# Keys of a cross-attention block: the order of the sums that end the keys' stage, and the power in two parts

## The chip, the cores and the metric

The kernel runs on one core of one Trainium2 chip. The metric is the time of the whole kernel on the device, in microseconds (us): the median over several runs. [...] Engines wait for each other by semaphores.

## What is computed

One block of a perceiver-like network on 128 rows `x` and 12544 context rows of width 512. Most of the time goes to the cross-attention to the context, of which this is the core:

```python
kvx = einsum('bsi,oi->bso', cond, w_kv_x)        # cond: the context, 12544 x 512
kx, vx = split(kvx, 2, axis=-1)                  # keys, values: 8 groups of 128 each
kx = ln(kx.reshape(b, sc, g, d), kxln_w, kxln_b) # a norm over the 128 of each key
xout = gqa(qx, kx, vx)                           # 16 query heads, 2 per group, softmax over the context
```

Around it stand a second attention of x to itself (with rounding to 8 bits), a projection of both, a causal self-attention, and a mixture of 32 experts with 8 chosen per row. The change touches only the cross-attention.

## The kernel before, in words

**Chunks.** The context is worked off in 25 chunks (0 to 24) of 512 tokens; chunk 12, in the middle, has 256. For each chunk there is a keys' stage (keys of the chunk into `KT`, with the outputs of the chunk before it on PE in between) and a values' stage (values into `V`, with the scores of the chunk in between). So on PE the order is: keys of chunk c with outputs of chunk c-1, values of chunk c with scores of chunk c, and so on. "Whole" chunks, all but 0 and 12, use the routine that is changed, `chunk_of`, for both stages (`k_chunk`, `v_chunk`).

**Products.** The 2x2 block product of mixed weights and mixed tokens is formed with seven products instead of eight (numbers 0 to 6), after Winograd's variant of Strassen. The outputs of a stage come in two units u, called the first and the second half: for the keys, groups 0 to 3 and groups 4 to 7; for the values, two sets of token tiles. Each unit has four output blocks `out(u, i, j)`. Of the seven products, 1, 3, 2 and 6 are split again by the same method into "quarters" that serve both halves at once: `pair(0, ..)` and `pair(1, ..)` are two generators of five steps each, in the banks 0, 1 and 2 of PSUM. Products 0, 5 and 4 are formed whole for each half, in a bank of their own for each half (`acc[u]`), and 0, 5 and 4 accumulate there: after each of them DVE adds the bank to its output block(s) (`add`, L332). So a bank can take its next product only when DVE has read the one before. ScalarE copies some quarters out of PSUM (`kept`, L329).

**Lower sums.** `out(u, 1, 0)` gets `out(u, 1, 1)` added on POOL (L522, one instruction for each half). The sum of product 4 writes `out(u, 1, 1)` afterwards, so it waits for that lower sum.

**The keys' norm.** After the last sum of a half, `k_sums` squares it on ScalarE (L594) and reduces the squares on DVE (L598); `k_rstd` folds the sums on DVE (L611, L617, L620) and raises to the power -0.5 on POOL (L622). The result `krs` scales the scores as ScalarE takes them out of PSUM (L941), so the first scores of a chunk can leave PSUM only when the first half's power is there. The scores' PSUM pool has three buffers.

**Other work in the queues.** POOL also mixes the next chunk's tokens (`mix_tokens`, L303 to L306, four instructions of 128x512, asked for after the last lower sum that the program has listed: `tc.issue_after(lower[0] or made)`), the finer mixtures (L445 to L448), and rescales the running outputs (L1028). DVE takes maxima of the scores (L949, L966, L976), subtracts them (L1013) and adds outputs (L1046). SP reloads the finer weights (`reload`, L432) and the context (L284).

**Order.** The program lists the stages' steps with generators: each step of `chunk_of` yields how many fills (pieces of outputs, or of scores) go after it. A build step then places the instructions on each engine; `tc.issue_after(x)` keeps what follows behind instruction x. For the keys, `keys` runs the fills and calls `k_sums` and `k_rstd`: the first half's fold is called after the first of the two closing steps, the second half's in the next stage (`after`, at g == 1).

Of the kernel before, what the change touches and what calls it, by code (L numbers as in the profile page):

```python
# [13 lines left out]
ALU = mybir.AluOpType  # L14
# [8 lines left out]
NH, G, D = 16, 8, 128  # L23
# [3 lines left out]
EPS = 1e-5  # L27
# [18 lines left out]
def block_kernel(  # L46
# [23 lines left out]
    nc = tc.nc  # L70
# [33 lines left out]
    mhalf = keep.tile([P, 16], F32, name="mhalf")  # L104
# [201 lines left out]
            lambda: eng.tensor_tensor(t4, b21, t2, ALU.subtract),  # L306
        ]

    mixed, last_mm, added, copied, lower = {}, [None], [None], [None], [None]
    aw = [[wkv[:, 0:2, o, :], wkv[:, 2:4, o, :]] for o in range(2)]  # L310
    mixed_w = (aw[0][0], aw[0][1], wsum[2], aw[1][1], wsum[0], wsum[1], aw[1][0])

# [12 lines left out]
    def bank(i):  # L325
        return (ps_kv if i < 3 else ps_kv3).tile([P, CH], F32, tag=f"kv{i}", name=f"kv{i}_ps")
# [156 lines left out]
    def chunk_of(v, c, fine, mm, view, to, pair_view, out, fills):  # L483


        def pair(p, banks):
            f = factors(c, v, p)
            return quarters(
                lambda ps, n, first: fine(f, ps, n, first), view, lambda i, j: to(p, i, j), banks
            )  # L490

        def reload(p):
            d = c if v == 0 else c + 1
            while d < NCH and not whole(d):
                d += 1
            if d < NCH and (1 - v, p) in kept_w:
                load_finer_weights(1 - v, p)

        acc = {}

        def main_part(u, i):
            if i == 0:
                acc[u] = bank((1, 3)[u])
            mm(acc[u], u, i, i == 0)
            if i == 4:
                add(out(u, 0, 1), pair_view(acc[u]))
                add(out(u, 1, 1), pair_view(acc[u]))
            else:
                add(out(u, i // 5, 0), pair_view(acc[u]))

        fills = iter(fills)
        for _ in pair(0, (1, 0, 2)):
            yield next(fills), None
        reload(0)
        extra = {1: (0, 0), 2: (1, 0), 3: (0, 5), 4: (1, 5)}
        for i, _ in enumerate(pair(1, (0, 1, 2))):
            if i in extra:
                main_part(*extra[i])
            if i == 4:
                reload(1)  # L520
                for u in range(2):
                    lower[0] = nc.gpsimd.tensor_tensor(  # L522
                        out(u, 1, 0), out(u, 1, 0), out(u, 1, 1), ALU.add
                    ).ins
            yield next(fills), None
        for u in range(2):
            main_part(u, 4)
            yield next(fills), u

    def k_chunk(c):  # L530

        h = CH // 2

        def fine(f, ps, n, first):
            for j in range(4):
                i, g = j // 2, j % 2
                nc.tensor.matmul(  # L537
                    ps[:, j * P : (j + 1) * P], lhsT=f[i][0][n][:, g * D : (g + 1) * D],
                    rhs=f[i][1][n], start=first and j == 0, stop=True, skip_group_check=True,
                )  # L540

        def mm(ps, u, i, first):
            w, x = mixed_w[i], mixed[c][i]
            for j in range(2):
                for k in range(2):
                    nc.tensor.matmul(  # L546
                        ps[:, j * h : (j + 1) * h],
                        lhsT=w[:, k, (2 * u + j) * D : (2 * u + j + 1) * D], rhs=x[:, k, :],
                        start=first and j == k == 0, stop=j == k == 1, skip_group_check=True,
                    )  # L550

        return chunk_of(
            0, c, fine, mm, lambda t: t.rearrange("p (g t) -> p g t", g=4),
            lambda p, u, v: KT[:, 4 * u : 4 * u + 4, p * h + v * P : p * h + (v + 1) * P],
            lambda t: t.rearrange("p (g t) -> p g t", g=2),
            lambda u, i, j: KT[:, 4 * u + 2 * i : 4 * u + 2 * i + 2, j * h : (j + 1) * h],
            (1, 1, 2, 1, 1, 1, 1, 1, 1, 1, 3, 2),
        )

    def v_chunk(c):  # L560

        def fine(f, ps, n, first):
            for i in range(2):
                nc.tensor.matmul(  # L564
                    ps[:, i * H // 2 : (i + 1) * H // 2], lhsT=f[i][1][n], rhs=f[i][0][n],
                    start=first and i == 0, stop=True, skip_group_check=True,
                )

        def mm(ps, v, i, first):
            w, x = mixed_w[i], mixed[c][i]  # L570
            for k in range(2):
                nc.tensor.matmul(  # L572
                    ps, lhsT=x[:, k, v * P : (v + 1) * P], rhs=w[:, k, H : 2 * H],
                    start=first and k == 0, stop=k == 1, skip_group_check=True,
                )

        return chunk_of(
            1, c, fine, mm, lambda t: t.rearrange("p (i g d) -> p i g d", i=2, d=D),
            lambda p, o, v: V[:, 2 * p + v].rearrange("p (i c g) d -> p i c g d", i=2, c=2)[
                :, :, o, :, :D  # L580
            ],
            heads, lambda v, i, j: v_out(2 * j + v, i),
            (1, 1, 2, 1, 1, 1, 1, 1, 1, 2, 2, 0),
        )

    def k_sums(c, u, pool):

        n = chunks[c][1]
        r = tmpk.tile([P, 4, CH // 32], F32, tag="sqr", name="sqr")
        for j in range(0, 4, 2):  # L590

            sq = pool.tile([P, CH // P, HS], F32, tag="s", name="sq", **({} if c else {"bufs": 1}))
            sq = sq.rearrange("p (g t) k -> p g (t k)", g=2)[:, :, :n]
            nc.scalar.activation(sq, KT[:, 4 * u + j : 4 * u + j + 2, :n], AF.Square)  # L594
            for i in range(1 if n == CH else 2):
                g = slice(j, j + 2) if n == CH else slice(j + i, j + i + 1)
                x = sq if n == CH else sq[:, i : i + 1, :]
                nc.vector.tensor_reduce(  # L598
                    r[:, g, : n // 32], x.rearrange("p g (b i) -> p g b i", i=32), AX.X, ALU.add,
                    apply_transpose=True,  # L600
                )
        return r

    def k_rstd(c, u, r):

        n, nt = chunks[c][1] // 32, chunks[c][1] // P


        w = tmpk.tile([32, 4, 4, CH // 32], F32, tag="kw", name="kw", bufs=1)
        for q in range(4):  # L610
            nc.vector.tensor_reduce(  # L611
                w[:, q, :, :n], r[32 * q : 32 * q + 32, :, :n, None], AX.X, ALU.add
            )
        ve = small.tile([P, 4, CH // P], F32, tag="kve", name="kve")
        wv = w.rearrange("p q g (t b) -> p g t b q", b=4)
        for b in range(4):
            nc.vector.tensor_reduce(  # L617
                ve[32 * b : 32 * b + 32, :, :nt], wv[:, :, :nt, b, :], AX.X, ALU.add
            )
        nc.vector.tensor_scalar(ve[:, :, :nt], ve[:, :, :nt], 1.0 / D, EPS, ALU.mult, ALU.add)  # L620
        rs = small.tile([P, 4, CH // P], F32, tag="krs", name="krs")
        nc.gpsimd.tensor_tensor(  # L622
            rs[:, :, :nt], ve[:, :, :nt],
            mhalf.rearrange("p (g t) -> p g t", g=4)[:, :, :nt], ALU.pow,
        )
        for g in range(4):
            rstds[c, 4 * u + g] = rs[:, g, :]

# [4 lines left out]
    def keys(c, fill, halves, squares):  # L633


        sums = {}
        if whole(c):
            due, given = 0, 0
            for n, unit_done in k_chunk(c):
                if unit_done is not None:  # L640
                    sums[unit_done] = k_sums(c, unit_done, squares)
                due += n
                while given < due * halves // 2:
                    next(fill)
                    given += 1
                if unit_done == 0:
                    k_rstd(c, 0, sums.pop(0))
            return sums
        for i, _ in enumerate(parts(k_unit(c, u) for u in range(2))):
            if i in (3, 7):  # L650
                sums[i // 7] = k_sums(c, i // 7, squares)
            for _ in range(halves):
                next(fill)
            if i == 6:
                k_rstd(c, 0, sums.pop(0))
        return sums
# [12 lines left out]
    with tc.tile_pool(name="pre", bufs=2) as pre, tc.tile_pool(name="pre1", bufs=1) as pre1, tc.tile_pool(  # L669
# [3 lines left out]
        for src, n in ((wqxT, 4), (wkT, 2), (wvT, 2), (wqT, 4)):  # L673
            v = src.rearrange("(k p) o -> p k o", p=P)
            stream += [v[:, :, i * H : (i + 1) * H] for i in range(n)]
        v = wprojT.rearrange("(b k p) o -> b p k o", p=P, k=NK)
# [233 lines left out]
        sums = first_sums(first_keys, sqp)  # L910
# [163 lines left out]
    for c in range(NCH):  # L1074
# [55 lines left out]
        if c + 1 < NCH:  # L1130
            fill = all_outputs()
            sums = keys(c + 1, fill, chunks[c][1] // HS, sp)
# [6 lines left out]
    with ExitStack() as rest:  # L1139
# [44 lines left out]
        c = NCH - 1  # L1184
# [329 lines left out]
```

## Time and profile before

| | us |
|---|---|
| median of 3 runs (lowest, highest) | 2200.26 (2199.98, 2200.66) |
| the profiled execution: time | 2197.91 |
| its span, first to last instruction | 2196.1 |
| PE busy | 2115.2 |
| DVE busy | 1544.2 |
| ACT busy | 936.9 |
| POOL busy | 709.5 |
| mean granted PE clock, as a share of full speed | 0.983 |

Times inside the execution are from the span's start. A line of a timeline gives start, length, engine, line, instruction, what it writes and reads, shapes, count, and in brackets the idle time before it with what ended it. A line of waits gives who waited for whom, the total, the number of times and the longest. A line of a group gives busy time and mean length in ns, and then the idle time before. A line of stretches gives from and to, then the busy time of PE, PEld, DVE, ACT and POOL, the granted clock, the share of the transfer engines, and GB/s. In the trace a whole chunk takes 76 to 78 us, and one full chunk's keys' stage runs from 850.70 to 888.28, its values' stage from there to 928.58.

### The profile page before, as it was taken

The numbers are of one execution on the slowest core, as the hardware profiler recorded it, in microseconds if no ns is written. First come the engines' busy times: TensorE is split into PE (matmuls) and PEld (weight loads), VectorE is DVE, ScalarE is ACT, GpSimd is POOL, SyncE is SP. The second block draws the span as 40 slices with busy tenths as digits, with TensorE's granted clock in tenths as the row PEclk, the third lists the DMA queues.
The fourth block names the chain that finished last, engine by engine and source line by source line (L and its number), as shares of the span: only waits on it lengthen the run. The fifth ranks groups of instructions, "written<-read, shape, count | busy, mean of one in ns | idle before, by whom it ended". The sixth has DMA issues, their size and how long they took to land.

```text
span 2196.1 us, 29775 instructions
## 1 busy us (share of the span) xinstructions
PE 2115.2 (96%) x11425; PEld 1709.5 (78%) x11425; DVE 1544.2 (70%) x2933; ACT 936.9 (43%) x1831; POOL 709.5 (32%) x888
## 2 busy tenths in 40 slices
PE   8999999999999999999999999999999999999999
PEld 4667887887887788787787887888788788776554
DVE  8787777678677767767777678777767867766311
ACT  3444454345445444444454445445434544542211
POOL 5325334324333422434334323333422433321000
PEclk9999999999999999999999999999999999999999
DMA  9311111021111111110111111111102111106693
GB/s 323 104 49 44 63 63 63 30 77 49 44 63 63 38 54 63 53 44 34 49 63 63 43 64 48 44 63 63 63 30 72 54 44 63 44 35 236 201 284 119
DMA packets 84494, 168.22 MB, mean 77 GB/s; under 512 B 4608, under 2 KB 40960, under 8 KB 84352
## 3 DMA queue, kind: packets, MB, share of 16 engines
q1 hardware_dynamic: 84064, 166.28, 22.1%
q8 instruction: 90, 1.47, 0.3%
q14 instruction: 52, 0.43, 0.1%
q10 hardware_dynamic: 288, 0.04, 0.0%
HBM read 162.90 MB, written 3.41 MB: 76 GB/s over the span
## 4 chain that ended last, share of the span: by engine, by line
PE 78%; DVE 10%; POOL 4%; ACT 4%; issue 2%; DMA 2%; SPq 0%; POOLq 0%; ACTq 0%; DVEq 0%
PE kv_ps L537 13%; PE s_ps L936 12%; PE kv_ps L564 12%; PE kv_ps L572 11%; PE o_ps L1039 10%; PE kv_ps L546 9%; PE gu_ps L1429 4%; POOL krs L622 3%; DVE sqr L598 3%; DVE KT L332 2%; PE moe_acc L1450 2%; ACT s L941 2%; PE ps_p L734 1%; PE kv_ps L366 1%; ACT sq L594 1%
## 5 line engine op out<-in xcount | busy, mean ns | idle before, releaser
L936 PE MATMUL s_ps<-qxT,KT 128*128 128x256 f32 x1568 | 391.9, 384 | 50.0 <-ACT s L941 50.0
L936 PEld LDWEIGHTS s_ps<-qxT,KT 128*128 128x128 f32 x1568 | 297.9, 192 | 152.1 <-ACT s L941 60.1
L941 ACT ACTIVATE s<-s_ps,krs 128x256 f32<-128x256 f32 x784 | 322.9, 471 | 203.6 <-PE s_ps L936 152.8
L332 DVE TENSOR_TENSOR KT<-kv_ps,KT 128x512 f32<-128x512 f32 (+1 forms) x334 | 226.6, 684 | 251.8 <-PE kv_ps L546 188.1
L1039 PE MATMUL o_ps<-V,s 128*128 128x129 f32 x3136 | 398.4, 276 | 1.3 <-ACT s L1026 0.7
L1039 PEld LDWEIGHTS o_ps<-V,s 128*128 128x128 f32 x3136 | 384.9, 192 | 9.9 <-ACT s L1026 1.4
L949 DVE TRANSPOSE_TENSOR_REDUCE mxr<-s 128x32 f32<-128x1024 f32 (+1 forms) x200 | 243.7, 1219 | 179.2 <-ACT s L941 179.2
L1026 ACT ACTIVATE s<-s 128x1024 f32<-128x1024 f32 (+1 forms) x200 | 202.4, 1038 | 121.9 <-DVE s L1013 118.5
L1028 POOL TENSOR_TENSOR ol<-ol,als 128x258 f32<-128x258 f32 x192 | 112.3, 616 | 409.5 <-ACT als L994 409.5
L1013 DVE TENSOR_TENSOR s<-s,b_ps 128x1024 f32<-128x1024 f32 (+1 forms) x200 | 232.0, 1190 | 1.7
L329 ACT COPY KT<-kv_ps 128x512 f32<-128x512 f32 (+1 forms) x196 | 112.6, 575 | 268.7 <-PE kv_ps L537 247.9
L332 DVE TENSOR_TENSOR V<-kv_ps,V 128x512 f32<-128x512 f32 x331 | 213.8, 668 | 14.4 <-PE kv_ps L564 10.9
L622 POOL TENSOR_TENSOR krs<-kve,mhalf 128x16 f32<-128x16 f32 (+1 forms) x50 | 143.0, 2860 | 246.0 <-DVE kve L620 245.9
L594 ACT ACTIVATE sq<-KT 128x1024 f32<-128x1024 f32 (+1 forms) x100 | 101.2, 1036 | 279.4 <-DVE KT L332 277.7
L522 POOL TENSOR_TENSOR KT<-KT 128x512 f32<-128x512 f32 x46 | 58.3, 1267 | 394.2 <-DVE KT L332 394.2
L546 PE MATMUL kv_ps<-mix,wsum 128*128 128x256 f32 x736 | 173.9, 379 | 0.0
L572 PE MATMUL kv_ps<-wsum,mix 128*128 128x512 f32 x368 | 172.9, 592 | 0.0
L546 PEld LDWEIGHTS kv_ps<-mix,wsum 128*128 128x128 f32 x736 | 132.9, 190 | 14.3
L329 ACT COPY V<-kv_ps 128x512 f32<-128x512 f32 x193 | 113.6, 589 | 39.7 <-PE kv_ps L564 21.6
L598 DVE TRANSPOSE_TENSOR_REDUCE sqr<-sq 128x32 f32<-128x1024 f32 (+1 forms) x104 | 117.0, 1164 | 7.9 <-ACT sq L594 7.9
L564 PE MATMUL kv_ps<-fw,fx 128*128 128x256 f32 x368 | 113.9, 464 | 1.4 <-ACT V L329 0.2
L572 PEld LDWEIGHTS kv_ps<-wsum,mix 128*128 128x128 f32 x368 | 69.9, 190 | 48.8 <-issue 44.0
(276 smaller groups left out, 3166.7 us busy)
## 6 DMA issues: line engine op xcount, KB each, us to landing
fw<-kept_w SPq DMA_DIRECT2D x88, 768.0 KB, 4.2
ctx<-in_ctxT SPq DMA_DIRECT2D x23, 1024.0 KB, 6.6
gu<-in_w SPq DMA_DIRECT2D x32, 384.0 KB, 5.1
gu<-in_v SPq DMA_DIRECT2D x32, 384.0 KB, 5.7
dn<-in_w SPq DMA_DIRECT2D x16, 768.0 KB, 5.7
w<-in_wprojT SPq DMA_DIRECT2D x8, 1024.0 KB, 5.5
w<-in_wqxT SPq DMA_DIRECT2D x4, 1024.0 KB, 11.3
w<-in_wqT SPq DMA_DIRECT2D x4, 1024.0 KB, 5.3
```

The lines of the kernel that those rows point to most:

```text
L329: copied[0] = nc.scalar.copy(dst, src).ins
L332: added[0] = nc.vector.tensor_tensor(dst, src, dst, ALU.add).ins
L537: nc.tensor.matmul(ps[:, j * P : (j + 1) * P], lhsT=f[i][0][n][:, g * D : (g + 1) * D], rhs=f[i][1][n], start=first and j == 0, stop=True, ...
L546: nc.tensor.matmul(ps[:, j * h : (j + 1) * h], lhsT=w[:, k, (2 * u + j) * D : (2 * u + j + 1) * D], rhs=x[:, k, :], start=first and j == k ...
L564: nc.tensor.matmul(ps[:, i * H // 2 : (i + 1) * H // 2], lhsT=f[i][1][n], rhs=f[i][0][n], start=first and i == 0, stop=True, skip_group_ch ...
L572: nc.tensor.matmul(ps, lhsT=x[:, k, v * P : (v + 1) * P], rhs=w[:, k, H : 2 * H], start=first and k == 0, stop=k == 1, skip_group_check=True,)
L622: nc.gpsimd.tensor_tensor(rs[:, :, :nt], ve[:, :, :nt], mhalf.rearrange("p (g t) -> p g t", g=4)[:, :, :nt], ALU.pow,)
L936: scored[0] = nc.tensor.matmul(ps[:, t - t0, :], lhsT=KT[:, g, t * P : (t + 1) * P], rhs=qxT[:, 2 * g : 2 * g + 2, :], start=True, stop=Tr ...
L941: copied[0] = nc.scalar.activation(s[:, t, :], ps[:, t - t0, :], AF.Copy, scale=rs[:, t : t + 1]).ins
L949: nc.vector.tensor_reduce(mxr[g // 4][:, g % 4, :nt, :].rearrange("p t k -> p (t k)"), s[:, :nt, :].rearrange("p t (k i) -> p (t k) i", i=32),
L1013: nc.vector.tensor_tensor(s[:, :nt, :], s[:, :nt, :], b[:, a, None, :].to_broadcast([P, nt, HS]), ALU.subtract,)
L1039: end = nc.tensor.matmul(ps[:, h, :], lhsT=s[:, t, h * S : (h + 1) * S], rhs=V[:, t, g, :], start=h == t == 0, stop=t == nt - 1, skip_grou ...
```

## The change

In `chunk_of`, for keys and values alike: the first half's product 0 is formed within the first pair of quarters (before its fourth step) and its sum after the fifth; its product 5 and the second half's product 0 are formed after the second and third step of the second pair. Then three steps close the stage: first half's product 4, second half's product 5, second half's product 4. The second half's product 5 thereby moves from before its lower sum to behind it. The banks of the two halves change places (first half bank 3, second half bank 1). In the keys the sums of the last step are placed behind the fold of the first half's squares (`folded[0]`, the last DVE instruction of `k_rstd`). `keys` calls the squares after the first and the third closing step, and the first half's fold after the second. The numbers of fills per step follow (13 steps instead of 12, the same sums: 16 and 14). In `k_rstd` the power is two instructions of two groups each instead of one of four; this holds for all chunks.

```diff
-        def main_part(u, i):
+        def product(u, i):
             if i == 0:
-                acc[u] = bank((1, 3)[u])
+                acc[u] = bank((3, 1)[u])
             mm(acc[u], u, i, i == 0)
+
+        def sums(u, i):
             if i == 4:
                 add(out(u, 0, 1), pair_view(acc[u]))
                 add(out(u, 1, 1), pair_view(acc[u]))
...
         fills = iter(fills)
-        for _ in pair(0, (1, 0, 2)):
+        quarter = pair(0, (1, 0, 2))
+        for i in range(5):
+            if i == 3:
+                product(0, 0)
+            next(quarter)
+            if i == 4:
+                sums(0, 0)
             yield next(fills), None
         reload(0)
-        extra = {1: (0, 0), 2: (1, 0), 3: (0, 5), 4: (1, 5)}
-        for i, _ in enumerate(pair(1, (0, 1, 2))):
-            if i in extra:
-                main_part(*extra[i])
+        quarter = pair(1, (0, 1, 2))
+        for i in range(5):
+            next(quarter)
+            if i in (1, 2):
+                product(i - 1, (5, 0)[i - 1])
+                sums(i - 1, (5, 0)[i - 1])
             if i == 4:
                 reload(1)
                 for u in range(2):
...
             yield next(fills), None
-        for u in range(2):
-            main_part(u, 4)
-            yield next(fills), u
+        for n, (u, i) in enumerate(((0, 4), (1, 5), (1, 4))):
+            product(u, i)
+            with tc.issue_after(folded[0]) if v == 0 and n == 2 else nullcontext():
+                sums(u, i)
+            yield next(fills), n
...
-            (1, 1, 2, 1, 1, 1, 1, 1, 1, 1, 3, 2),
+            (1, 1, 1, 1, 1, 1, 1, 1, 1, 1, 1, 3, 2),
...
-            (1, 1, 2, 1, 1, 1, 1, 1, 1, 2, 2, 0),
+            (1, 1, 1, 1, 1, 1, 1, 1, 1, 1, 1, 2, 1),
...
-        nc.vector.tensor_scalar(ve[:, :, :nt], ve[:, :, :nt], 1.0 / D, EPS, ALU.mult, ALU.add)
+        folded[0] = nc.vector.tensor_scalar(
+            ve[:, :, :nt], ve[:, :, :nt], 1.0 / D, EPS, ALU.mult, ALU.add
+        ).ins
         rs = small.tile([P, 4, CH // P], F32, tag="krs", name="krs")
-        nc.gpsimd.tensor_tensor(
-            rs[:, :, :nt], ve[:, :, :nt],
-            mhalf.rearrange("p (g t) -> p g t", g=4)[:, :, :nt], ALU.pow,
-        )
+        for g in range(0, 4, 2):
+            nc.gpsimd.tensor_tensor(
+                rs[:, g : g + 2, :nt], ve[:, g : g + 2, :nt],
+                mhalf.rearrange("p (g t) -> p g t", g=4)[:, g : g + 2, :nt], ALU.pow,
+            )
...
-            for n, unit_done in k_chunk(c):
-                if unit_done is not None:
-                    sums[unit_done] = k_sums(c, unit_done, squares)
+            for n, at in k_chunk(c):
+                if at in (0, 2):
+                    sums[at // 2] = k_sums(c, at // 2, squares)
+                elif at == 1:
+                    k_rstd(c, 0, sums.pop(0))
                 due += n
                 while given < due * halves // 2:
                     next(fill)
                     given += 1
-                if unit_done == 0:
-                    k_rstd(c, 0, sums.pop(0))
```

More of the change, by code (lines that the diff above doesn't have):

```diff
@@ L307, in mix_tokens @@
         ]
-    mixed, last_mm, added, copied, lower = {}, [None], [None], [None], [None]
+    mixed, last_mm, added, copied, lower, folded = {}, [None], [None], [None], [None], [None]
     aw = [[wkv[:, 0:2, o, :], wkv[:, 2:4, o, :]] for o in range(2)]
```

## The prediction, made before the changed kernel ran

> **What bounds the kernel now.** I read the page's shares first, then the waits of TensorE (PE), then one chunk's timeline on each engine.
>
> ```profile
> PE 2115.2 (96%) x11425; PEld 1709.5 (78%) x11425; DVE 1544.2 (70%) x2933; ACT 936.9 (43%) x1831; POOL 709.5 (32%) x888
> ```
>
> PE is the bound. So the change can win only what PE loses in idle time and clock, and loses whatever new waits it gives PE. The waits have one large row:
>
> ```profile
> PE s_ps L936 <- ACT s L941: 50.0, 24, 3.1
> ```
>
> In PE's timeline this is one stop per chunk, early in the values' stage, at the third piece of scores:
>
> ```profile
> 873.78 0.61 PE L537 MATMUL kv_ps<-fx,wkv 128*128 128x128 f32 x4
> 874.23 1.89 PE L546 MATMUL kv_ps<-mix,wsum 128*128 128x256 f32 x8
> ...
> 891.30 0.59 PE L564 MATMUL kv_ps<-wkv,mix 128*128 128x256 f32 x2
> 893.97 1.44 PE L936 MATMUL s_ps<-qxT,KT 128*128 128x256 f32 x4 [2.07 <-ACT s L941]
> ```
>
> The chain of waits at the next chunk says what is late (start, length): the fold of the first half's squares, then the power, then ScalarE's scaling.
>
> ```profile
> 962.00 2.37 DVE sqr L598 x2
> ...
> 968.04 2.92 POOL krs L622
> 970.96 0.02 issue
> 970.98 1.57 ACT s L941 x4
> ```
>
> The stretches around that stop show a second price; the granted clock is the third figure from the end.
>
> ```profile
> 890.00:894.00 4.00, 1.93 (x10) 1.36 (x8) 2.65 (x4) 1.98 (x4) 2.91 (x1) 1.00 0.00 0
> 894.00:898.00 4.00, 4.00 (x11) 2.94 (x12) 3.22 (x9) 2.55 (x6) 0.00 (x0) 0.58 0.00 0
> 898.00:902.00 4.00, 4.00 (x20) 3.54 (x19) 2.18 (x5) 2.21 (x5) 2.91 (x1) 0.99 0.00 0
> ```
>
> After the stop the clock halves for some 3.4 us. Third scores pieces follow each other 78.15 us apart where that happens (350.53 to 428.67) and 76.45 where not (506.81 to 583.25), so it costs 1.69 us. Of the 21 stops of 2.08 it followed 16.
>
> Last, POOL's queue at the end of the keys' stage:
>
> ```profile
> 878.71 1.27 POOL L522 TENSOR_TENSOR KT<-KT 128x512 f32<-128x512 f32 x1 [18.18 <-DVE KT L332]
> 880.51 1.27 POOL L522 TENSOR_TENSOR KT<-KT 128x512 f32<-128x512 f32 x1 [0.53 <-DVE KT L332]
> 881.73 1.27 POOL L303 TENSOR_TENSOR mix<-ctx 128x512 f32<-128x512 f32 x1
> 883.08 1.29 POOL L304 TENSOR_TENSOR mix<-ctx,mix 128x512 f32<-128x512 f32 x1
> 884.32 1.28 POOL L305 TENSOR_TENSOR ctx<-ctx 128x512 f32<-128x512 f32 x1
> 885.56 1.28 POOL L306 TENSOR_TENSOR mix<-ctx,mix 128x512 f32<-128x512 f32 x1
> ```
>
> Both lower sums (L522; first half's first) stand ahead of the four mixes of the next chunk's tokens.
>
> **Keys: what goes.** The first half's last product now ends with three outputs' halves (0.89 each), a product (1.73), a product and two halves, two scores pieces and two quarters (0.86 each) behind it; 12.3 us, where it was 9.6. The chain from it takes 11.7 (960.16 to 971.87). So taken alone, the 2.08 stop would go.
>
> **Keys: what comes.** The second half's sum of product 5 is now behind its lower sum, so that lower sum no longer waits for it and is ready first, after the copy of the last-but-one quarter. The mixes wait only for "the second half's lower sum". In the changed program's order POOL therefore has: second half's lower sum, four mixes, first half's lower sum, powers. And the first half's last sum (product 4 into the right half's lower groups) has to wait for the first half's lower sum, which reads what it overwrites. Count from E, the end of PE's last-but-one quarter (874.23 above):
>
> - ScalarE's copy starts at E+0.20 (874.43) and takes 0.58; POOL 0.08 later, E+0.86. One lower sum, 1.22 to the next start; four mixes 5.11 (881.73 to 886.84); the other lower sum 1.27: E+8.46.
> - DVE's last sum starts at E+8.5; the second square 0.73 after (as 882.29 to 883.02) and ends 1.0 later, E+10.25. The two reductions (2.37 a pair) stand ahead of the sum of product 5 of the second half in DVE's order: second reduction from 10.3 to 11.5, that sum (0.69) to E+12.2.
> - That sum reads the bank into which the second half's product 4 adds. PE reaches it at E + 0.89x3 + 1.73x2 + 0.89 + 2.68 = E+9.70 and waits until 12.25.
>
> So a stop of 2.55 takes the place of the 2.08. Without the handover lags and at the smallest pitches it is 1.6; with 0.15 more on each of three handovers 3.0. I keep 2.55, which is worked from this chunk's own rows. Later the fold (sums 0.86 and 1.05, two outputs' additions) ends by E+14.8, the first power by 16.5. The new wait of the last sums for the fold holds them to 16.1 and, on ScalarE ahead of the scores, two squares to 17.55; PE wants its third scores piece at E+19.2, and the first scaled pair is out at 18.4. That cover is 0.8 us; with it gone each us late costs PE a us. The split power costs POOL 2x1.645-2.91, 0.4 us, by these rows, under the same cover:
>
> ```profile
> L622 POOL TENSOR_TENSOR krs<-kve,mhalf 128x16 f32<-128x16 f32 x48 | 139.7, 2911 | 239.9 <-DVE kve L620 239.8
> L622 POOL TENSOR_TENSOR krs<-kve,mhalf 128x8 f32<-128x8 f32 x2 | 3.3, 1645 | 6.1 <-DVE kve L620 6.1
> ```
>
> **Which chunks.** The order has this shape in 19 of 23 full chunks (2 to 10, 14 to 23). Chunk 1 has two mixes and three weight sums of 0.73 between its lower sums: about 1.7, where it lost 3.06. Before the short chunk the mixes are half as long (0.73): 0.2. Chunk 13 has two mixes between (its sum is in time) and lost 2.99; chunk 24 has none. These three lost a slow clock each too.
>
> **Values: the same routine.** DVE sets this stage's end. Before, the fourth group's row maximum started here, and the last subtraction ended 14.45 us later, where the second row starts:
>
> ```profile
> 828.52 1.25 DVE L949 TRANSPOSE_TENSOR_REDUCE mxr<-s 128x32 f32<-128x1024 f32 x1 [1.04 <-ACT s L941]
> ...
> 842.97 1.28 DVE L332 TENSOR_TENSOR V<-kv_ps,V 128x512 f32<-128x512 f32 x2
> ```
>
> Its steps were mxr 1.17, add 0.57, maxima 1.52+1.54+0.68, transpose 0.76, subtraction 1.14, add 0.6, subtraction 1.13, mxr 1.16, two adds 1.17, transpose 0.74, two subtractions 2.27. In the changed order the stretch from that row maximum to the second half's sum of product 5 holds: mxr 1.17, maxima 3.74, six adds 3.6, two transposes 1.5, four subtractions 4.53, two mxr 2.32 and the sum itself: 17.55, and it starts 1.07 after PE ends that group's scores. PE's order from that end to the second half's product 4 is five quarters, seven and a half scores pieces and four products (1.72): 17.67. The same bank makes it wait 1.0 (0.5 to 1.5: 0.03 on each of some seventeen steps, either way). Halts of 0.72 and 1.05 (148.81, 79.88) left the clock at 1.00, so no clock is charged.
>
> At the keys' start only 0.67, not 0.89, of output stands between a quarter and the next in its bank, and the copy takes 0.2+0.58: 0.1 per chunk. The reloads of the finer weights keep their place in SP's queue, and the quarter that frees their buffer ends within 2 us of where it did, far from their use: nothing. In the short chunk and in chunk 0 only the power is split. At chunk 0 it starts at 106.1 and the first scores at 125.9: nothing. In the short chunk two powers of 128x4 (1.41 each in the projections' norms) replace one of 1.645; POOL stands idle for 4.45 after the first weight step behind the second power (1041.34 to 1046.52), so nothing again, 1 at most.
>
> **Clock.** A 2.55 stop should slow the clock at least as often as 2.08 did; the longer ones do not agree (2.99 did; 3.06 and 3.55 did not). I take 0.8 of 19, 15.2 against 14 of these 19 before. [...]
>
> **Sum**, in us: 19 x (2.55-2.08) = +8.9; clock 1.2 x 1.69 = +2.0; chunk 1 -1.4; chunk 11 0.2-3.77 = -3.6; chunk 13 -4.7; chunk 24 -3.8; values 23 x 1.0 = +23.0; keys' start +2.3. Together +22.7 on the profiled execution (2197.9, span 2196.1), 2220.6. That execution lies 2.35 below the median of the runs, so 2223.
>
> **Rivals.**
> 1. The lower sum is not what decides: faster. Place: DVE's last sum of the first half. Price: the keys' stops go, -39.5 (19 x 2.08) -23.7 (14 slow clocks) -13.5 (the four odd chunks), with the values' stage and the keys' start +25.3: about 2149. It decides if that sum can start by E+5.9. For it: without POOL's order it would start at E+5.2. Against: four mixes lie between, 5.11 in this trace, and their data landed long before (transfer issued at 842.66).
> 2. The values' stop is covered: +22.7-23, no change, 2200. For it: DVE idled 2.14 near the end of that stage (848.12). Against: that was after the sums; PE's wait lies before.
> 3. Both stops larger, the values' 2.0 with half of them slowing the clock: +23 and 11 x 1.7, 2265. For it: 1.0 and 2.08 are near. Against: the price is summed from rows that repeat to 0.02.
>
> **Chances and range.** Forecast 0.72 (its ends, added as squares: keys 19 x -0.95 or +0.45, values 23 x 0.5 either way, four slow clocks either way; 2201 to 2240), rival 1 0.10, rival 2 0.10, rival 3 0.08. Leaving out rival 1 and the larger part of rival 3, the range is 2195 to 2250. Changes under 0.2% (4.4 us) can't be told from none. Faster: rival 1 and 0.03 of rival 2. Same: 0.05 of rival 2 and 0.02 of the forecast's low end. Slower: the rest.
>
> **What would show it.** Right: PE's keys products waiting for DVE's KT sums some 2.5 us in 19 chunks and the values' products some 1 us in 23; the wait for ScalarE's scaling nearly gone; DVE's KT sum waiting 3.3 us for POOL; a lower sum after the mixes. Wrong: no PE wait for DVE, or mixes that start late.

## The result, and the profile after

The changed kernel takes 2205.22 us (median of 8 runs), the kernel before 2199.82 on the same chip: a ratio of 1.0035, with a 95% interval of 1.0024 to 1.0046. It is slower, as forecast, but by 5.4 us where some 23 were forecast (2223). The profiled execution has a span of 2203.2 us, 7.1 more than before; the forecast for this difference was 22.7.

The page's shares, the line to set beside the first one of the kernel before (PE is TensorE and PEld its weight loads, DVE is VectorE, ACT ScalarE, POOL GpSimd):

```profile
PE 2109.9 (96%) x11425; PEld 1698.5 (77%) x11425; DVE 1563.2 (71%) x2933; ACT 940.1 (43%) x1831; POOL 723.0 (33%) x938
```

The waits of PE (total, times, longest):

```profile
PE kv_ps L558 <- DVE KT L332: 44.4, 20, 2.2
PE kv_ps L584 <- DVE V L332: 15.1, 23, 0.7
...
PE kv_ps L576 <- DVE KT L332: 0.8, 1, 0.8
...
PE s_ps L951 <- ACT s L956: 0.4, 1, 0.4
```

The wait for ScalarE's scaling (50.0 before) is gone but for one of 0.4. In its place stand the keys' products waiting for DVE's sums, in 20 chunks, and the values' products waiting for the same, in 23. Both were forecast. The chain of waits, in order of time, shows the whole mechanism of the keys' stop in one chunk (start, length, what):

```profile
802.49 1.27 POOL KT L532
803.75 1.24 POOL mix L303
804.99 0.07 issue
805.06 1.27 POOL mix L304
806.33 1.23 POOL ctx L305
807.56 1.23 POOL mix L306
808.79 1.23 POOL KT L532
810.02 0.02 issue
810.04 0.69 DVE KT L332
810.73 2.37 DVE sqr L610 x2
813.10 0.59 DVE KT L332
813.69 0.04 issue
813.73 1.99 PE kv_ps L558 x8
```

First the second half's lower sum (L532), then the four mixes of the next chunk's tokens, then the first half's lower sum (L532) behind them, then DVE's last sum of the first half, the two reductions of squares, the sum of product 5, and only then PE's product. DVE's own waits give the first link its total:

```profile
DVE KT L332 <- POOL KT L532: 64.5, 22, 3.1
```

Where the 7.1 us come from can be counted from PE's record. Take the start-to-start distance of two matmuls, and take off what it usually is for that line (0.112 us for an output, 0.216 for a score, 0.429 for a values' product): what is left was lost. Distances during a slow clock are kept apart, and the waits that the profile names are taken from its list.

| in the chunks | before | after | change | forecast |
|---|---|---|---|---|
| keys' stops, as the waits show them | 50.0 | 45.6 | -4.4 | +0.5 |
| values' stops, as the waits show them | 0 | 15.1 | +15.1 | +23.0 |
| losses under 0.5 us each | 16.3 | 23.8 | +7.5 | +2.3 (keys' start) |
| slow clock, in the whole span | 33.7 | 20.9 | -12.8 | -3.1 |
| sum | | | +5.4 | +22.7 |

The forecast column is its own terms sorted into these rows: 8.9 - 1.4 - 1.9 - 3.0 - 2.1 for the keys' stops (the three odd chunks without their clocks), and 2.0 - 3 x 1.69 for the clock. The remaining 1.7 us lie outside the chunks. Every row is off by 5 to 10 us, and the largest single miss is the clock.

### The profile page after: what moved, and what is told of

Read it like the earlier page. It is cut to its first block, busy times and chain, and to the rows that moved or that the text cites. A ratio compares the mean times of both kernels' runs of the same rounds, so it can differ in the third digit from the quotient of the medians.

```text
span 2203.2 us, 29960 instructions
## 1 busy us (share of the span) xinstructions
PE 2109.9 (96%) x11425; PEld 1698.5 (77%) x11425; DVE 1563.2 (71%) x2933; ACT 940.1 (43%) x1831; POOL 723.0 (33%) x938
## 3 DMA queue, kind: packets, MB, share of 16 engines
q1 hardware_dynamic: 84064, 166.28, 22.5%
## 4 chain that ended last, share of the span: by engine, by line
PE 60%; DVE 24%; POOL 7%; issue 5%; ACT 2%; DMA 1%; POOLq 0%; SPq 0%; DVEq 0%; ACTq 0%
PE kv_ps L549 12%; PE o_ps L1054 9%; PE s_ps L951 8%; PE kv_ps L576 8%; PE kv_ps L558 7%; DVE s L1028 5%; DVE V L332 4%; DVE mxr L964 4%; PE kv_ps L584 4%; PE gu_ps L1444 4%; POOL KT L532 2%; DVE sqr L610 2%; PE moe_acc L1465 2%; DVE KT L332 2%; DVE m_new L991 2%
## 5 line engine op out<-in xcount | busy, mean ns | idle before, releaser
L1054 PE MATMUL o_ps<-V,s 128*128 128x129 f32 x3136 | 405.3, 276 | 0.8 <-ACT s L1041 0.8
L332 DVE TENSOR_TENSOR V<-kv_ps,V 128x512 f32<-128x512 f32 x331 | 218.4, 677 | 95.3 <-ACT V L329 51.2
L637 POOL TENSOR_TENSOR krs<-kve,mhalf 128x8 f32<-128x8 f32 (+1 forms) x100 | 160.3, 1620 | 305.7 <-DVE kve L632 305.7
L558 PE MATMUL kv_ps<-mix,wsum 128*128 128x256 f32 x736 | 190.7, 406 | 44.6 <-DVE KT L332 44.4
L558 PEld LDWEIGHTS kv_ps<-mix,wsum 128*128 128x128 f32 x736 | 142.3, 204 | 66.5 <-DVE KT L332 48.8
L584 PE MATMUL kv_ps<-wsum,mix 128*128 128x512 f32 x368 | 175.3, 599 | 15.1 <-DVE V L332 15.1
L532 POOL TENSOR_TENSOR KT<-KT 128x512 f32<-128x512 f32 x46 | 58.3, 1267 | 321.5 <-ACT KT L329 320.9
L549 PE MATMUL kv_ps<-fx,fw 128*128 128x128 f32 x736 | 91.8, 277 | 5.3 <-ACT KT L329 4.3
```

The lines of the kernel that those rows point to most:

```text
L332: added[0] = nc.vector.tensor_tensor(dst, src, dst, ALU.add).ins
L549: nc.tensor.matmul(ps[:, j * P : (j + 1) * P], lhsT=f[i][0][n][:, g * D : (g + 1) * D], rhs=f[i][1][n], start=first and j == 0, stop=True, ...
L558: nc.tensor.matmul(ps[:, j * h : (j + 1) * h], lhsT=w[:, k, (2 * u + j) * D : (2 * u + j + 1) * D], rhs=x[:, k, :], start=first and j == k ...
L584: nc.tensor.matmul(ps, lhsT=x[:, k, v * P : (v + 1) * P], rhs=w[:, k, H : 2 * H], start=first and k == 0, stop=k == 1, skip_group_check=True,)
L1054: end = nc.tensor.matmul(ps[:, h, :], lhsT=s[:, t, h * S : (h + 1) * S], rhs=V[:, t, g, :], start=h == t == 0, stop=t == nt - 1, skip_grou ...
```

## The experiments

Two questions were open: whether each stop has the cause that was forecast, and what sets apart the 9 of 19 keys' stops of 2.24 us that a slow clock followed, where it had followed 16 of 21 stops of 2.08.

**POOL's order.** The two lower sums are emitted in the other order, so that the mixes wait for the first half's:

```diff
-                for u in range(2):
+                for u in (1, 0):
                     lower[0] = nc.gpsimd.tensor_tensor(
```

The order of the instructions on PE, DVE and ScalarE is the same as in the changed kernel; POOL alone differs.

> The changed kernel with one thing different: the two lower sums are emitted second half first, so that the mixes of the next chunk wait for the first half's lower sum, and POOL does both lower sums ahead of the four mixes. Theory (POOL's order makes the keys' stop): in the profile after the change DVE's last sum of the first half waits 3.12 us for POOL in every full chunk and PE then 2.24 us for DVE (44.4 in 20 stops); with both lower sums first the sum can start 3 us earlier and these stops go, and the slow clocks behind nine of them. Span 2203.2 - 44 - 9 x 1.7 = 2144 or some us less, if a stop also costs a restart. Rival A (DVE's order makes it: the two reductions of squares ahead of the second half's sum of product 5): stops of 1.5 us or more stay in the same place, span above 2175. Rival B (what is late next takes over): the power, now with the mixes still ahead of it on POOL, makes PE wait at the third scores piece, 1 us or more a chunk, span 2165 or more.

Measured: ratio 0.9735 (0.9718 to 0.9751), span 2140.8. PE's waits for the keys' sums are gone from the list but for one of 0.4, and its first row of the chunks is the values' 15.1:

```profile
PE kv_ps L584 <- DVE V L332: 15.1, 23, 0.7
```

In POOL's timeline of this kernel the second lower sum now follows 0.63 after the first, when its data are there, and DVE's two last sums run as one pair:

```profile
554.07 1.27 POOL L532 TENSOR_TENSOR KT<-KT 128x512 f32<-128x512 f32 x1 [15.05 <-ACT KT L329]
555.97 1.27 POOL L532 TENSOR_TENSOR KT<-KT 128x512 f32<-128x512 f32 x1 [0.63 <-DVE KT L332]
```

```profile
557.82 1.29 DVE L332 TENSOR_TENSOR KT<-kv_ps,KT 128x512 f32<-128x512 f32 x2 [1.24 <-PE kv_ps L558]
```

So one instruction's place in POOL's queue was the whole keys' stop. Rivals A and B are out: DVE still has the squares' reductions ahead of the sum of product 5, and PE does not wait for the power either. From one chunk to the next without a slow clock PE now takes 75.21 us instead of 77.72.

**The keys' order without the values', and the values' without the keys'.** In the next kernel the values' stage calls the routine of before, in the one after it both edits are made, in the last the kernel of before has the changed routine in its values' stage alone:

```diff
-        return chunk_of(
+        return chunk_of_old(
             1, c, fine, mm, ...
-            (1, 1, 1, 1, 1, 1, 1, 1, 1, 1, 1, 2, 1),
+            (1, 1, 2, 1, 1, 1, 1, 1, 1, 2, 2, 0),
```

> The changed kernel with the values' stage put back to the order of before; the keys as changed. The values' stops (15.1 us in 23) should go. Between two chunks without a slow clock PE's period is 76.45 before and 77.71 after, 1.26 more, of which the two kinds of stops show only 0.82 (2.24 - 2.08 and 0.66); if the rest, 0.44, belongs to the values' order, the period here is 76.6, if to the keys', 77.05. Slow clocks, theory G (the clock is set for steps of 3.413 us on a fixed grid, by the idle time of the step before, at about 1.65 us): a chunk of 76.6 carries the 2.24 stop through the grid so that some 17 of 19 are followed by a slow clock, and the span is 2203.2 - 25 + 8 x 1.7 = 2192. Rival (the share of slow clocks goes by the kind or length of the stop): 9 of 19 as after the change, 2178; or 0.76 as before, 14 to 15 of 19, 2187.

> Both edits together: POOL does both lower sums of the keys ahead of the mixes, and the values' stage has the order of before. If the keys' stop is POOL's order and the values' stop is the values' order, no stop is left in the full chunks and no slow clock: 2196.1 - 50 - 17 x 1.7 = 2117 for the span, down to 2109 if each stop also costs 0.35 for its restart. Rivals as with the first of these kernels: the keys' stops stay (above 2150), or PE waits for the power at the third scores piece (above 2140).

> The kernel of before with the changed order in the values' stage alone. It measures the values' order by itself: stops of 0.66 in 23 chunks for the sum of product 5, +15 us, or +25 if the 0.44 a chunk that the two kinds of stops leave open belongs to the values too. The keys' stops of 2.08 stay. Slow clocks by theory G at a period of 77.45: some 13 of 21, four less than before: 2196.1 + 25 - 7 = 2214. By a fixed share they would stay at 17: 2221.

Measured: keys alone 0.9872 (0.9858 to 0.9887), span 2168.7; both edits 0.9559 (0.9544 to 0.9574), span 2097.1; values alone 1.0093 (1.0078 to 1.0108), span 2219.3. The kernel with both edits is the fastest of all. It is 12 to 20 us below the 2117 to 2109 that were expected; the keys' order gains at two handovers besides (below), 0.6 a chunk or 14 us. PE's share shows it:

```profile
PE 2065.3 (98%) x11425; PEld 1686.7 (80%) x11425; DVE 1546.4 (74%) x2933; ACT 932.1 (44%) x1831; POOL 726.0 (35%) x938
```

Period of a chunk without a slow clock, and number of slow steps of 3.413 us in the chunks:

| kernel | period, us | slow steps |
|---|---|---|
| before | 76.45 | 17 |
| after | 77.72 | 9 |
| keys' order alone | 76.01 | 11 |
| values' order alone | 78.17 | 7 |
| after, both lower sums first | 75.21 | 0 |
| keys' order alone, both lower sums first | 73.51 | 0 |

The periods add up: the keys' order is worth -0.44 a chunk even with its stop, the values' order +1.72, both together 76.45 - 0.44 + 1.72 = 77.73 where 77.72 was measured. With the lower sums first two of the periods fall by 2.51 and 2.50. The numbers of slow steps do not add up: each order alone takes six or ten away, both together eight. Of the keys' stops 11 of 19 were followed by one with the keys alone and 5 of 21 with the values alone, which neither theory had (17, or 9, or 14 to 15; 13, or 17); the experiment on the clock below comes back to these counts. The span of the values alone, 2219.3, lies near the 2221 of a fixed share by luck: the period was longer than supposed (78.17, not 77.45) and the slow steps were fewer.

The values' 1.72 is far more than the 0.66 that the waits show. In the kernel with both lower sums first the losses of one chunk between 526 and 602 are: 0.40 where a quarter waits for ScalarE's copy, 0.92 at the stop (0.82, and 0.10 at the first matmul behind it), 0.45 at the start of the next keys; 1.77 in all. With the values' order of before these three are absent. So the 0.44 that the two kinds of stops left open was the values', and more than that; the period of the keys alone was neither 76.6 nor 77.05, because the keys' order gains besides. In the timeline of the changed kernel they are three short rows:

```profile
684.77 0.70 PE L576 MATMUL kv_ps<-wsum,fx 128*128 128x256 f32 x2
...
695.60 1.99 PE L584 MATMUL kv_ps<-wsum,mix 128*128 128x512 f32 x4 [0.66 <-DVE V L332]
...
700.91 2.02 PE L549 MATMUL kv_ps<-fx,fw 128*128 128x128 f32 x16
```

Only the middle one carries a wait. The first, a quarter, starts 0.3 late behind scores that started at 683.61 and take 0.86; ScalarE shows why, since its copy stands behind two small instructions that wait for DVE's maxima:

```profile
683.67 0.44 ACT L1009 ACTIVATE als<-dfs 32x8 f32<-32x8 f32 x2 [1.54 <-DVE dfs L1004]
684.13 0.59 ACT L329 COPY V<-kv_ps 128x512 f32<-128x512 f32 x1
```

The keys' side has the opposite: two handovers that cost 0.34 and 0.28 a chunk before (a quarter behind the stop, another late in the keys) are gone, all but 0.08, with the keys' order alone, which is how a stop of 2.24 in place of 2.08 goes with a shorter period.

**DVE's backlog in the values' stage.** The kernel with both lower sums first, with one subtraction fewer:

```diff
-        for a in range(2):
+        for a in range(1 if whole(c) and j == 0 else 2):
             s = prob[2 * j + a]
```

> The kernel with the mixes behind both lower sums and the values' order as changed, with one of DVE's eight subtractions of the row maxima (1.14 us) left out in each full chunk; the output is then wrong for that group. PE's order differs by one scores matmul and by the place of two output matmuls at the keys' start. In that kernel a chunk of 75.21 us loses three times: 0.40 where a quarter waits for ScalarE's copy ahead of the subtraction left out, 0.92 at the stop for the sum of product 5, 0.45 at the start of the keys. Theory (DVE's backlog behind the row maxima makes the two later ones): they go, the quarter's stays, a period of some 74.0 and a span of 2141 - 23 x 1.2 = 2113. Rival (the exchanged banks make the keys' start wait, whatever DVE does): 0.45 stays, 74.4, 2123.

Measured: ratio 0.9663 (0.9635 to 0.9691), span 2123.4, period 74.52. The stop for the sum of product 5 falls from 0.92 to 0.33, while PE reaches it 0.43 earlier by the other order of its scores; together 1.02 of the 1.14 of the subtraction that is gone. So this stop is DVE's backlog. The quarter's 0.40 stays, as both theories had it. At the keys' start 0.28 of 0.45 stays. That part is not DVE's backlog alone: it would fit the exchanged banks (the last product of the values now lies in bank 1, which the first quarters of the keys use), but the banks were not tried by themselves, so its cause stays open. The period of 74.52 lies above what either theory had (74.0 and 74.4).

**Power in two parts, and the fold.** Each undone in the kernel with both edits.

```diff
-        for g in range(0, 4, 2):
-            nc.gpsimd.tensor_tensor(
-                rs[:, g : g + 2, :nt], ve[:, g : g + 2, :nt], ...
+        nc.gpsimd.tensor_tensor(
+            rs[:, :, :nt], ve[:, :, :nt], ...
```

```diff
-            with tc.issue_after(folded[0]) if v == 0 and n == 2 else nullcontext():
-                sums(u, i)
+            sums(u, i)
```

> The kernel with both edits (mixes behind both lower sums, values' order of before), with the power in one instruction of four groups again. In the profile of that kernel the first half's power starts at 556.98, ScalarE is free of the squares at 559.50, its first pair of scalings is out by 560.44, and PE wants the bank at 561.46. The whole power takes 2.91: scalings from 559.91, out by 560.85, 0.6 ahead of PE. Theory: nothing changes, within 0.1% of 0.9559 of the kernel of before. Rival (the power in two parts is what takes the wait for ScalarE away): PE waits at the third scores piece by up to 1.3 us a chunk, 10 to 30 us more.

> The kernel with both edits, with the last sums of the keys not tied to the fold of the first half's squares. The fold is emitted ahead of these sums in any case; of DVE's rows the order changes in one chunk only. Theory: within 0.1% of the kernel with both edits. Rival (the fold's place decides over the stop): one or more stops of 1 us come back in most chunks, over 20 us.

Measured: 0.9579 (0.9563 to 0.9595) with the power whole, 0.9566 (0.9552 to 0.9580) without the wait for the fold, beside 0.9559 (0.9544 to 0.9574). The intervals overlap. With the power whole the profile has one more wait at the third scores piece, in chunk 1 (0.63); the one of 0.36 near the short chunk stands in all three kernels (0.35 to 0.36). Neither rival holds: in the kernel with both edits the two parts of the change differ from it by 0.2% and 0.07%. In the changed kernel itself they were not undone.

**The clock.** In the traces the slow clock comes in steps of 3.413 us (near the ends of an execution up to three in a row, 10.240), and every slow step of one execution begins at a whole multiple of 3.4133 us from every other (to within 0.001 us for the 20 slow stretches of the kernel before and the 12 after). So the slow steps of a trace lie on one grid, and a stop can lie in one step of it or be shared by two. To move the stops through the grid without touching them, the kernel of before was given useless matmuls early in the keys, two in one kernel and six in another:

```diff
             w, x = mixed_w[i], mixed[c][i]
+            for _ in range(6 if first and u == 0 else 0):
+                nc.tensor.matmul(
+                    ps[:, :h], lhsT=w[:, 0, 2 * u * D : (2 * u + 1) * D], rhs=x[:, 0, :],
+                    start=True, stop=False, skip_group_check=True,
+                )
```

> The kernel of before with two useless matmuls of 0.216 us more in each full chunk's keys (the first one of the first half's product 0 is done three times, with the same outcome). PE's period without a slow clock goes from 76.45 to 76.88. Theory G (clock steps of 3.413 us on a fixed grid; a step is slow when PE stood idle for some 1.65 us or more within the step before): carrying a stop of 2.08 through the grid at that period gives a slow clock after 20 of 21 instead of 16 or 17: 2196.1 + 23 x 0.43 + 3.5 x 1.69 = 2212 for the span. Rival (a fixed share of the stops): 2206.

> The same with six useless matmuls, 1.30 us: a period of 77.75 without a slow clock. Theory G: some 10 of 21 slow: 2196.1 + 23 x 1.30 - 7 x 1.69 = 2214 for the span, no more than 2 or 3 us above the kernel with two. Rival (a fixed share): 2226, 20 us above.

Measured: 1.0086 (1.0071 to 1.0101) with two, span 2216.2, and 1.0217 (1.0197 to 1.0237) with six, span 2247.7. The expectations had the price of a matmul wrong by half (one call is two rows of the profile, 0.44 us), so the periods are 77.34 and 79.07, and neither number of the expectations can be compared as it stands. The stops stayed as they were (50.2 us in 24 in both), and the slow clock followed 18 of the 21 stops of 2.08 us with two matmuls, 8 of 21 with six. A fixed share is out. The counts are of one profiled execution each, and belong to it rather than to the kernel: of the four runs with six more matmuls one took 2240.28 at a granted clock of 0.993, the profiled one 2249.49 at 0.988. By these figures that is an estimated six or seven slow steps fewer (0.005 of 2245 us, at half of 3.413 a step). Two stops of 2.09 us of the kernel with six, cut at the grid (which is laid 0.05 us ahead of the starts of the slow steps; each line gives the stretch, its length, busy time and number of PE, PEld, DVE, ACT, POOL, then the granted clock):

```profile
833.59:837.01 3.42, 2.86 (x14) 2.18 (x12) 3.39 (x6) 1.46 (x2) 2.31 (x1) 1.00 0.01 2
837.01:840.42 3.41, 1.80 (x7) 1.30 (x8) 1.38 (x3) 2.76 (x7) 0.60 (x1) 1.00 0.00 0
840.42:843.83 3.41, 3.41 (x18) 3.00 (x17) 2.91 (x12) 1.88 (x5) 0.58 (x1) 1.00 0.00 0
...
915.51:918.93 3.42, 1.25 (x6) 0.78 (x5) 1.40 (x3) 2.19 (x6) 1.18 (x1) 1.00 0.02 5
918.93:922.34 3.41, 3.41 (x9) 2.67 (x10) 3.15 (x11) 1.28 (x3) 0.03 (x1) 0.51 0.00 0
```

The first stop is shared by two steps (PE busy for 2.86 and 1.80), and the clock stays at 1.00. The second lies in one step (1.25), and the next step is slow (0.51). The same in the changed kernel, at two keys' stops of 2.24:

```profile
809.36:812.78 3.42, 2.13 (x20) 1.94 (x18) 2.74 (x3) 1.06 (x1) 0.65 (x1) 1.00 0.00 0
812.78:816.19 3.41, 2.46 (x14) 2.25 (x15) 3.26 (x12) 0.00 (x0) 0.00 (x0) 1.00 0.00 0
816.19:819.60 3.41, 3.41 (x23) 3.15 (x23) 2.82 (x6) 2.49 (x4) 3.10 (x2) 1.00 0.00 0
...
887.87:891.28 3.41, 1.33 (x12) 1.14 (x11) 3.41 (x4) 1.06 (x1) 0.00 (x0) 1.00 0.00 0
891.28:894.70 3.42, 3.26 (x8) 2.63 (x9) 2.70 (x12) 0.00 (x0) 0.49 (x1) 0.51 0.00 0
```

And in the kernel of before, at the stop that ends at 506.81, which two steps share:

```profile
502.08:505.49 3.41, 2.66 (x13) 2.00 (x11) 3.38 (x6) 1.26 (x2) 2.51 (x1) 1.00 0.00 0
505.49:508.91 3.42, 2.02 (x8) 1.49 (x9) 1.40 (x3) 2.88 (x7) 0.40 (x1) 1.00 0.00 0
508.91:512.32 3.41, 3.41 (x18) 3.00 (x17) 2.90 (x11) 1.97 (x4) 0.81 (x1) 1.00 0.00 0
```

Over the 11 profiled kernels of this case, from 160 us to 1940 us, there are 5725 grid steps. Each of the 75 that a slow step follows lost 2.13 us or more of PE's time, counted as in the table of the result; none of the other 5650 lost more than 2.11. The traces of the kernel before and of the changed one give both ends: 2.13 in the step from 427.0 before, 2.11 in the step from 184.7 after. This sharp line hangs on the 0.05 us: with the grid at the starts of the slow steps themselves the two kinds overlap between 2.08 and 2.16, so in these traces they part at 2.1 to within some 0.05. The measure that the expectations used, 1.65 us of the shown wait, does not hold: 1.63 in one step was enough in the kernel of before, and 1.99 was not in the one with two more matmuls. The two kinds part only when what is lost beside the shown wait is counted with it. What sets the clock was not shown; these are counts.

An estimate from these figures, one stop carried through a grid of 3.4133 us at the measured period with 1.69 us added after each slow step and the line at 2.1, gives 16 of 21 before (16 in the trace), 9 of 19 after (9), 10 of 19 with the keys' order alone (11), 5 of 21 with the values' alone (5) and 7 of 21 with six more matmuls (8). With two more, where a slow step cost 1.36 (periods of 78.70 and 77.34), it gives 18 (18). Where in the grid the first stop is put moves these counts by one or two. With the values alone a slow step cost 1.35 as well (79.52 and 78.17); with that the count is 4 to 7. Why a slow step cost less in these two kernels stays open.

## Why the prediction was right or wrong

- **Direction and mechanism: right.** The prediction's rows for POOL's queue, DVE's sum and PE's product came as named: the chain of waits above is its list, step for step. Rival 1 (the lower sum does not decide) and rival 2 (the values' stop is covered) are refuted by the stops and by the run with both lower sums first. That run is what rival 1 described, and took 2141.22 us where rival 1 said 2149. The nearness is part luck, since the values' order cost more than the 25.3 in it and the keys' handovers gained what it did not have. That the changed kernel came out slower is part luck too: the misses below add up to -15.6 of the 22.7.
- **"So a stop of 2.55 takes the place of the 2.08": 2.24.** In the chunk whose chain is shown, PE's last-but-one quarter ends at 801.62 (E). DVE's sum of product 5 released PE at E+12.11, where 12.25 was forecast, and PE reached the place at E+9.87, where 9.70 was. Two misses of 0.15 each on the two sides of a difference; 19 x 0.31 = 5.9 us. The chunk counts were right but for chunk 13, where 0.8 remained.
- **"The same bank makes it wait 1.0": 0.66,** within its bounds, 7.9 us less in 23 chunks. But the place was counted as the values' only loss. The order costs 1.72 a chunk, 40 us in 23: the quarter behind ScalarE's copy and the start of the keys cost another 0.85, of which the prediction had 0.1, at "the keys' start".
- **"Nothing" for the handovers in the keys: -0.6 a chunk.** The prediction went from stop to stop and did not list the losses under 0.3 us that the page's waits leave out. They are in the start times: 0.34 and 0.28 a chunk that the new order removes.
- **"I take 0.8 of 19" slow clocks: 9 of 19.** This step failed most. It took the share of slow clocks as a property of the stop's length, and 2.55 for "at least as often" as 2.08. The trace of before has the answer already: with the slow steps of that trace laid on one grid, the five stops of 2.08 without a slow clock are those that two steps share, with 1.51 us or less of the stop in either; of the other 16 each has 1.63 or more in one step. At a period of 77.72 instead of 76.45 the stops meet the grid otherwise, and fewer lie in one step: after the change PE lost 2.15 us or more in one step at each of the nine, and 1.77 or less in either step at the other ten. Worth 6.2 x 1.69 = 10.5 us, the largest error. The granted clocks of the other runs agree: 0.982 to 0.986 before, 0.987 to 0.990 after. The trace's warning stood in the prediction itself: "the longer ones do not agree".
- **The power in two parts and the wait for the fold** were costed at nothing under a cover of 0.8 us. In the kernel with both edits the runs without them moved the time by 0.2% at most; under that cover, in the changed kernel, they were not undone. In the short chunk the two powers of 128x4 take 1.01 each, not the 1.41 that the prediction took from another place; no wait hung on it.

The sum of 22.7 thus was too high by 9.7 for the clock, 4.9 for the keys' stops and 7.9 for the values', and too low by 5.2 for the small losses and 1.7 outside the chunks: 22.7 - 22.5 + 6.9 = 7.1.

## What to carry to other kernels

When an ordered wait ("after the last of these") stands for a set, look which member is last once the order changes: here the same line, with its loop turned round, makes 0.9735 out of 1.0035, and 0.9559 if the values keep their old order. Cost a reordering at every handover of the stage, from start-to-start distances, not only at the stops that the waits name. And where stops repeat with a period, see in the trace where each lies among the slow steps before counting on a share of slow clocks: here a changed period alone made it 18 of 21 (two more matmuls, 77.34) or 8 of 21 (six more, 79.07) in place of 16 (76.45).

## What the runs showed of the hardware that was not expected

In the traces of this case the slow clock went with what PE had lost in the 3.4133 us before it. A loss of 2.13 us or more of 3.413 was followed by half clock (0.50 or 0.51) in the next step, one of 2.11 or less by full clock (0.99 or 1.00), in 5725 steps of 11 kernels without an exception if the grid is laid 0.05 us ahead of the slow steps' starts, and with a blur of 2.08 to 2.16 if it is laid on them. A slow step cost 1.69 us of time in the kernel before, 1.35 with the values' order alone and 1.36 with two more matmuls. Stops shown as 2.08 us lay on both sides of that line, and by where it fell the same stop cost its 2.08 or, with 1.69 more, 3.77: 5 of 21 were followed by a slow step at a period of 78.17 (the values' order alone), 18 of 21 at 77.34 (two more matmuls).

In the changed kernel a matmul behind a stop started its next one 0.10 us later than usual (0.320 where 0.216 is usual at the keys' stops without a slow clock, 0.533 where 0.429 is at the values'), and the last one before it showed 0.16 of its end as busy time (0.275 where its pitch is 0.112, 0.379 where it is 0.216), so that a wait shown as 0.66 cost 0.92 and one of 2.24 cost 2.5. The times of the changed kernel lie in two groups, 2204.1 to 2205.5 and 2209.0 to 2209.4; their granted clocks are 0.990 and 0.987. The 4.4 us between the groups would be two or three slow steps of 1.69, an estimate from these figures; the second group was not profiled.
